# Moving group-norm sums to TensorE, a positional sum to GpSimd, and turning two matrix products around

## The chip, the cores and the metric

The kernel runs on one NeuronCore of a Trainium2 chip. Times are device microseconds of one execution. A core has five engines with a queue each: TensorE (PE in the profile, with PEld for its weight loads), VectorE (DVE), ScalarE (ACT), GpSimd (POOL) and SyncE (SP), which here issues every DMA. Each queue runs in program order, and engines wait for one another by semaphores. On-chip memory is SBUF (128 partitions) and PSUM, into which matmuls write.

## The reference, cut to what matters

The input is x, 16 images of 256 channels and 32 x 32 positions, float32. Two layers follow, each on a group-normalised input and each added to x:

```python
x = x + attention_block(_gn(x), ...)   # layer norm, 4 heads, feed-forward
x = x + mamba_block(_gn(x), ...)
```

The group norm works on the array as it is laid out in memory, with the last axis split into 16 groups of two columns: mean and variance are over all channels, all rows and the two columns of a group.

```python
g = v.reshape(B_, H_, W_, G, C_ // G)          # G = 16
m = jnp.mean(g, axis=(1, 2, 4), keepdims=True)
```

The second block adds a positional term (rel_h + rel_w), computes a gate ctx as the sigmoid of a 3-tap convolution over 256 channels, projects to u and z (512 channels each), convolves and activates u, computes delta, B and C from it, and runs a scan of 1024 steps over 512 channels with 64 states each. Then y = (ys + u * D) * silu(z), a product of y with out_proj_w gives 256 channels, and the result times ctx is taken from [position, channel] order straight into [channel, row, column] by a reshape (not by a transpose), and is added to x.

## The kernel before, in words

Channels lie on the partitions (KC = 2 blocks of 128), positions along the free axis (L = 1024, in halves of HL = 512). The scan is cut into 4096 units (256 per image): a unit is 2 channels x 64 states on 128 partitions and 1024 steps. For each unit n the main loop emits `load` (a DMA of du, broadcast, six units ahead), `inputs` (GpSimd's product with B, L956, four units ahead), pieces of `outputs` (TensorE's sums over the states, L998 and L1010, with ScalarE's copies L1004 and L1014), `scan(n)` (VectorE, L973) and `decay(n + 2)` (TensorE L965, then ScalarE's exponential L967, into a PSUM buffer of which there are two).

Everything else of the kernel is side work, woven in between the units. `prepare(b + 1)` (first norm, attention layer, scan inputs of the next image) and `gate_and_store(b - 1)` (gating, output product and store of the image before) are generators. They yield a share after every step; `rate_for` finds a rate at which the shares of one image fill its 256 units (a share below 1 isn't stretched or squeezed, and a larger one never gets below one unit). In a unit the side steps come after `scan(n)` and `decay(n + 2)`, and the last lines of the kernel fix the order of each engine's queue as it was emitted. For the first image `prepare(0)` runs before the loop, and the last `gate_and_store` runs after it. In images with both, the order of the side work is: first norm, gate_and_store, attention layer, scan inputs.

Five places matter here. `group_norm` is used twice per image, in `first_norm` and in `scan_inputs`: VectorE reduces each of the two channel blocks to 16 group sums (L274), TensorE sums these over the partitions with a constant matrix (L279), VectorE subtracts (L293), ScalarE squares (L295), the squares are summed in the same way, ScalarE turns the variance into a factor by Ln and Exp (L305, L306), and VectorE multiplies (L309). After the second norm VectorE adds the positional term (L657), and the first readers of the sum are the z products (L680). `layer_norm` (L317) already sums over channels by matmuls with a constant matrix as weights and the values as the moving operand.

`gate` computes the convolution of ctx. Its result is needed in the order of the final reshape, in which row r of the output holds four positions of 256 channels. So it takes every fourth position as the 128 columns of the weights (`xp[k][:, ds(first + t, P, 4)]`) and the 256 output channels as the moving operand, in quarters (q) of a PSUM bank, and adds the bias by a matmul of one row (L730, L736); tanh follows (L739). The output product in `gate_and_store` does the same with `us` and `wo_s` (L910), and two VectorE operations apply the gate and add x (L897, L899).

`psum` and `psum3` give PSUM banks; beside the scan there are two (`mm`) and, for `psum3`, a third (`accp`). `work` and `hwork` give SBUF tiles of 1024 and 512 columns, from 10 and 4 buffers.

## Time and profile before

| | us |
|---|---|
| median of 3 runs | 12651.92 (12599.05 to 12653.68) |
| the profiled execution | 12609.29 |
| its span, first to last instruction | 12607.5 |
| VectorE busy | 11264.3 (89%) |
| GpSimd busy | 10030.6 (80%) |
| TensorE busy, matmuls | 9517.2 (75%) |
| TensorE busy, weight loads | 5493.8 (44%) |
| ScalarE busy | 7523.0 (60%) |
| mean granted clock of TensorE | 0.799 of full |

A row of the groups reads: line, engine, operation, what it writes <- what it reads, shapes, x count | busy us, mean ns of one | idle us of the engine just before them, and what ended most of it. A row of the timeline reads: start us, duration us, engine, line, operation, x count of merged instructions, and in brackets the idle time before with its releaser. A float32 matmul has two records, so 1464 + 72 records of L730 are 768 matmuls, 48 for each of 16 images. Busy times of TensorE are modelled at their ends. A row of the waits reads: who waited <- for whom: us in total, times, the longest.

### The profile page before, as it was taken

The numbers are of one execution on the slowest core, as the hardware profiler recorded it, in microseconds if no ns is written. First come the engines' busy times: TensorE is split into PE (matmuls) and PEld (weight loads), VectorE is DVE, ScalarE is ACT, GpSimd is POOL, SyncE is SP. The second block draws the span as 40 slices with busy tenths as digits, with TensorE's granted clock in tenths as the row PEclk, the third lists the DMA queues.
The fourth block names the chain that finished last, engine by engine and source line by source line (L and its number), as shares of the span: only waits on it lengthen the run. The fifth ranks groups of instructions, "written<-read, shape, count | busy, mean of one in ns | idle before, by whom it ended". The sixth has DMA issues, their size and how long they took to land.

```text
span 12607.5 us, 421113 instructions
## 1 busy us (share of the span) xinstructions
PE 9517.2 (75%) x184752; PEld 5493.8 (44%) x184752; DVE 11264.3 (89%) x7482; ACT 7523.0 (60%) x10758; POOL 10030.6 (80%) x4201
## 2 busy tenths in 40 slices
PE   6676876868778687786878768687686877868777
PEld 2344444444444444444444444444444444444445
DVE  2799999899999899898998999999999998989998
ACT  3565655656656565565656656565565665656554
POOL 0587878878788787887878878788887878878798
PEclk7887977878878697887878878797787978878755
DMA  1566667676676766767666676766767667676676
GB/s 53 178 224 239 220 214 239 221 244 219 216 238 227 245 216 223 240 219 245 226 223 235 220 240 221 241 219 222 237 224 247 217 223 241 221 245 217 230 250 231
DMA packets 1070137, 2819.91 MB, mean 224 GB/s; under 512 B 324162, under 2 KB 402243, under 8 KB 1068292
## 3 DMA queue, kind: packets, MB, share of 16 engines
q1 hardware_dynamic: 1068292, 2792.97, 65.0%
q8 instruction: 1444, 23.66, 0.8%
q14 instruction: 401, 3.28, 0.1%
HBM read 2513.82 MB, written 261.62 MB: 220 GB/s over the span
## 4 chain that ended last, share of the span: by engine, by line
DVE 37%; PE 32%; issue 13%; ACT 8%; DMA 7%; POOL 3%; SPq 1%; DVEq 0%; POOLq 0%; ACTq 0%
DVE h L973 27%; PE yb L998 6%; PE a L965 5%; ACT a L967 4%; DMA dub<-dus 3%; PE av L531 3%; POOL dub L956 3%; PE st_ps L543 3%; DVE over L449 2%; PE z_ps L680 2%; PE s_ps L469 2%; PE g_ps L730 2%; PE yb L1010 1%; PE m_ps L910 1%; DVE u L716 1%
## 5 line engine op out<-in xcount | busy, mean ns | idle before, releaser
L956 POOL TENSOR_TENSOR dub<-dub,bt 128x1024 f32<-128x1024 f32 x4096 | 9805.4, 2420 | 2446.0 <-DMA dub<-dus 2241.7
L973 DVE TENSOR_TENSOR_SCAN h<-a,dub 128x1024 f32<-128x1024 f32 x4096 | 9176.7, 2275 | 705.4 <-ACT a L967 406.0
L967 ACT ACTIVATE a<-a,acol 128x1024 f32<-128x1024 f32 x4096 | 4464.1, 1090 | 3157.7 <-PE a L965 3092.6
L965 PE MATMUL a<-pieces,pick 48*128 48x512 bf16 x8192 | 1914.0, 458 | 2473.6 <-DVE h L973 2362.0
L998 PEld LDWEIGHTS yb<-h,cd 128*32 128x32 f32 x131072 | 2496.9, 128 | 2639.8 <-issue 1332.2
L998 PE MATMUL yb<-h,cd 128*32 128x64 f32 x131072 | 3266.9, 252 | 342.4 <-ACT y L1004 234.8
L965 PEld LDWEIGHTS <-pick 48*128 48x128 bf16 x8192 | 597.0, 95 | 2886.7 <-issue 2256.4
L1004 ACT COPY y<-yb 128x256 f32<-128x256 f32 x2048 | 763.3, 373 | 598.5 <-PE yb L998 589.1
L531 PE MATMUL av<-pt,vv 128*64 128x512 f32 x2048 | 607.7, 674 | 2.9 <-ACT sums L520 1.6
L551 ACT ACTIVATE pt<-st_ps 128x512 f32<-128x512 f32 x1024 | 552.9, 597 | 82.9 <-PE st_ps L543 82.0
L1010 PE MATMUL yb<-turn,y 128*32 128x16 f32 x32768 | 590.1, 214 | 2.3 <-issue 1.2
L543 PE MATMUL st_ps<-sp 33*128 33x512 f32 x2048 | 583.2, 646 | 2.9 <-ACT pt L551 2.9
L1010 PEld LDWEIGHTS yb<-turn,y 128*32 128x32 f32 x32768 | 571.7, 159 | 2.6 <-ACT y L1004 1.4
L730 PE MATMUL g_ps<-w,xp 128*128 128x256 f32 x1464 | 457.0, 452 | 0.1
L1014 ACT COPY yo<-yb 128x128 f32<-128x128 f32 x512 | 135.3, 264 | 519.1 <-PE yb L1010 510.9
L730 PEld LDWEIGHTS g_ps<-w,xp 128*128 128x128 f32 x1464 | 368.7, 326 | 67.7 <-issue 58.7
L469 PE MATMUL s_ps<-kd,qm 64*128 64x512 f32 x1022 | 367.5, 617 | 14.0 <-DVE kd L444 7.5
L449 DVE CUSTOM_DVE_ANT_0 over<-s_ps,over 128x512 f32<-128x512 f32 x512 | 326.8, 676 | 24.4 <-PE s_ps L469 24.4
L910 PE MATMUL m_ps<-w,xs 128*128 128x256 f32 x1024 | 321.6, 464 | 11.4 <-POOL xs L885 11.4
L716 DVE SCALAR_TENSOR_TENSOR u<-up,cwh,u 128x1024 f32<-128x1024 f32 x192 | 302.7, 1576 | 27.9 <-ACT u L708 27.7
L477 ACT ACTIVATE over<-s_ps 128x512 f32<-128x512 f32 x511 | 275.3, 595 | 32.8 <-PE s_ps L469 32.8
L910 PEld LDWEIGHTS m_ps<-w,xs 128*128 128x128 f32 x1024 | 262.9, 328 | 59.3 <-issue 26.7
(180 smaller groups left out, 7126.8 us busy)
## 6 DMA issues: line engine op xcount, KB each, us to landing
dub<-dus SPq DMA_DIRECT2D x4096, 512.0 KB
dps<-pc SPq DMA_DIRECT2D x384, 128.0 KB
pieces<-dps SPq DMA_DIRECT2D x1024, 48.0 KB
xs<-in_x_dram SPq DMA_DIRECT2D x64, 512.0 KB
xs<-kept SPq DMA_DIRECT2D x64, 512.0 KB
zs<-z SPq DMA_DIRECT2D x64, 512.0 KB
ud<-u SPq DMA_DIRECT2D x64, 512.0 KB
dus<-du SPq DMA_DIRECT2D x64, 512.0 KB
```

Of the source, the lines that this page charges most:

```text
L469: nc.tensor.matmul(s, qm[c // NJ][r, c % NJ], keys[r], start=True, stop=True)
L531: nc.tensor.matmul(av[ts(e, 2 * DH)], vv[j // (NJ // 2)][:, j % (NJ // 2), 2 * pair + e, :], pts[e], start=(j == 0), stop=(j == NJ - 1),)
L543: nc.tensor.matmul(s, ka[r, ts(j, P)], qa[r, hs(hf)], start=True, stop=True)
L730: nc.tensor.matmul(ps[:, ts(q, C)], xp[k][:, ds(first + t, P, 4)], wg_s[:, k, t, :], start=(k == 0 and t == 0), stop=False,)
L910: nc.tensor.matmul(ps[:, ts(q, C)], us[d][:, ds(first, P, 4)], wo_s[:, d, :], start=(d == 0), stop=(d == ND - 1),)
L956: nc.gpsimd.tensor_tensor(v, v, blocks[units[n][0]]["bt"], ALU.mult)
L965: nc.tensor.matmul(a[:, hs(hf)], w, pieces[r], start=True, stop=True)
L967: nc.scalar.activation(a, a, AF.Exp, scale=acol[:, at : at + 1])
L973: nc.vector.tensor_tensor_scan(now["h", e][:, i, :], decays.pop(n), loaded.pop(n), 0.0, ALU.mult, ALU.add)
L998: nc.tensor.matmul(yb[ts(g, 32), ts(s, 64)], cd[:, at // 16, ts(c, 32)], hbuf[:, :, at : at + 8], start=(c == 0), stop=(c == 1),)
L1004: nc.scalar.copy(y2[:, r], yb[:, :256])
L1010: nc.tensor.matmul(some[ts(r, 32), x], y2[:, r, x:256:8], turn[:, x], start=True, stop=True)
```

## The change

The group norm's sums are made by TensorE: a constant matrix (1 / the number of values in a group) is the weights and the values themselves move, so that a PSUM bank collects 512 column sums over all channels and both halves; one VectorE reduction over the bank then gives the 16 group values. ScalarE copies the mean back into the bank, and the constant factor moves into the matrix. The mean has a step of its own, so that the norm has ten steps in place of nine. The preload of the table set ahead of Ln is gone.

The positional sum after the second norm is issued on GpSimd.

The gate product now holds a 128 x 128 block of the gate's weights and moves 512 positions, so its result lies as [channel, position]; the bias comes in with the activation. The output product is turned around likewise, and since the result must still end in the order of the reshape, `join` multiplies projection and gate into an SBUF tile, and `turn_back` brings it to that order by matmuls with the identity, with every fourth position as weights. The eight steps of the stage alternate between projections ("p") and turns ("t").

```diff
--- before.py
+++ after.py
@@ -140,14 +140,15 @@
         assert i + n <= w
         return vec[:, o + i : o + i + n]
 
-    gate_b = const.tile([1, C], F32, name="gate_b")
-    nc.sync.dma_start(gate_b, gate_bias)
-    one_row = const.tile([1, P], F32, name="one_row")
-    nc.vector.memset(one_row, 1.0)
+    gate_b = const.tile([P, KC], F32, name="gate_b")
+    nc.sync.dma_start(gate_b, gate_bias.rearrange("o (k p) -> p (o k)", p=P))
+    nc.vector.tensor_scalar(gate_b, gate_b, 0.5, None, ALU.mult)
     ident = const.tile([P, P], F32, name="ident")
     make_identity(nc, ident)
     avg = const.tile([P, P], F32, name="avg")
     nc.vector.memset(avg, 1.0 / C)
+    share = const.tile([P, P], F32, name="share")
+    nc.vector.memset(share, 1.0 / (C * L / NG))
     eps = const.tile([P, 1], F32, name="eps")
     nc.vector.memset(eps, 1e-5)
 
@@ -269,40 +270,43 @@
 
 
     def group_norm(src, dst):
-        def sum_of(part, s, k):
-            view = part.rearrange("p (h g t) -> p g h t", g=NG, t=2)
-            nc.vector.tensor_reduce(s[:, k, :], view, AX.XY, ALU.add)
-
-        def mean_of(s, name):
-            m = psum(f"{name}_ps")[:, :NG]
-            for k in range(KC):
-                nc.tensor.matmul(m, avg, s[:, k, :], start=(k == 0), stop=(k == KC - 1))
+        def sum_of(part, sums, k):
+            for h in range(2):
+                nc.tensor.matmul(
+                    sums, share, part[:, hs(h)],
+                    start=(k == 0 and h == 0), stop=(k == KC - 1 and h == 1),
+                )
+
+        def mean_of(sums):
+            m = small.tile([P, NG], F32, name="gn_s", tag="gn_s")
+            nc.vector.tensor_reduce(
+                m, sums.rearrange("p (h g t) -> p g h t", g=NG, t=2), AX.XY, ALU.add
+            )
             return m
 
-        per = C / (C * L / NG)
-        s = small.tile([P, KC, NG], F32, name="gn_s", tag="gn_s")
+        s = psum("gn_m_ps")
         sum_of(src[0], s, 0)
         yield 1
         sum_of(src[1], s, 1)
-        m = mean_of(s, "gn_m")
-        yield 1
-        s = small.tile([P, KC, NG], F32, name="gn_q", tag="gn_s")
+        yield 1
+        m = s[:, :NG]
+        nc.scalar.copy(m, mean_of(s))
+        yield 1
         qs = []
-        nc.vector.tensor_scalar(m, m, per, None, ALU.mult)
         for k in range(KC):
             nc.vector.tensor_tensor(grouped(dst[k]), grouped(src[k]), over_group(m), ALU.subtract)
             q = work("gn_sq")
             nc.scalar.activation(q, dst[k], AF.Square)
             qs.append(q)
             yield 1
+        s = psum("gn_v_ps")
         sum_of(qs[0], s, 0)
         yield 1
         sum_of(qs[1], s, 1)
         del qs, q
-        v = mean_of(s, "gn_v")
-        yield 1
-        table("log")
-        nc.scalar.activation(v, v, AF.Ln, bias=eps, scale=per)
+        yield 1
+        v = s[:, :NG]
+        nc.scalar.activation(v, mean_of(s), AF.Ln, bias=eps)
         nc.scalar.activation(v, v, AF.Exp, scale=-0.5)
         yield 2.2
         for k in range(KC):
@@ -654,7 +658,7 @@
         )
         del xs
         for k in range(KC):
-            nc.vector.tensor_tensor(body[k], body[k], rels[k], ALU.add)
+            nc.gpsimd.tensor_tensor(body[k], body[k], rels[k], ALU.add)
             yield 0.6
         del rels
 
@@ -719,24 +723,22 @@
 
         gates = {}
 
-        def gate(o, hf, q, k):
-            if (hf, q, k) == (0, 0, 0):
+        def gate(o, hf, part):
+            if (hf, part) == (0, 0):
                 gates["g"] = work("g")
-            if (q, k) == (0, 0):
+            if part == 0:
                 gates["ps"] = psum("g_ps")
             g, ps = gates["g"], gates["ps"]
-            first = o * HL + hf * 2 + q
-            for t in range(3):
+            for at in ((0, 1), (2,), (3, 4), (5,))[part]:
+                k, t = divmod(at, 3)
                 nc.tensor.matmul(
-                    ps[:, ts(q, C)], xp[k][:, ds(first + t, P, 4)], wg_s[:, k, t, :],
-                    start=(k == 0 and t == 0), stop=False,
+                    ps, wg_s[:, k, t, ts(o, P)], xp[k][:, ds(hf * HL + t, HL)],
+                    start=(at == 0), stop=(at == 5),
                 )
-            if k < KC - 1:
-                return
-            nc.tensor.matmul(ps[:, ts(q, C)], one_row, gate_b, start=False, stop=True)
-            if q == 1:
-                table("tanh")
-                nc.scalar.activation(g[:, hs(hf)], ps, AF.Tanh, scale=0.5)
+            if part == 3:
+                nc.scalar.activation(
+                    g[:, hs(hf)], ps, AF.Tanh, scale=0.5, bias=gate_b[:, o : o + 1]
+                )
                 if hf == 1:
                     nc.sync.dma_start(gs[ts(o, P), :], g)
 
@@ -754,16 +756,16 @@
             tap(d, 2)
             table("tanh")
             nc.scalar.activation(ups[d][:, :L], us[d], AF.Tanh)
-            gate(d // 2, d % 2, 0, 0)
+            gate(d // 2, d % 2, 0)
             yield 1
-            gate(d // 2, d % 2, 0, 1)
+            gate(d // 2, d % 2, 1)
             yield 1.5
             nc.vector.scalar_tensor_tensor(us[d], ups[d][:, :L], 1.0, us[d], ALU.add, ALU.mult)
             ups[d] = None
             nc.sync.dma_start(ud[ts(d, P), :], us[d])
-            gate(d // 2, d % 2, 1, 0)
+            gate(d // 2, d % 2, 2)
             yield 1
-            gate(d // 2, d % 2, 1, 1)
+            gate(d // 2, d % 2, 3)
             yield 1.5
         gates.clear()
         del xp, body
@@ -890,35 +892,54 @@
                 yield 0.4
         if b + 2 < B:
             come += fetches(state[b + 2].setdefault("tok", []), state[b + 2]["kept"])
-        ready = []
+        turned, gated = [], {}
 
         def finish():
-            for o, hf, ps in ready:
-                nc.vector.scalar_tensor_tensor(ps, gs[o][:, hs(hf)], 1.0, ps, ALU.add, ALU.mult)
+            for o, hf, ps in turned:
                 t = xs[o][:, hs(hf)]
                 nc.vector.scalar_tensor_tensor(t, ps, 0.25, t, ALU.mult, ALU.add)
                 if hf == 1:
                     nc.sync.dma_start(out[b, ts(o, P), :], xs[o])
-            ready.clear()
-
-        for o in range(KC):
-            for hf in range(2):
-                ps = psum3("m_ps")
-                for q in range(2):
-                    first = o * HL + hf * 2 + q
-                    for d in range(ND):
-                        nc.tensor.matmul(
-                            ps[:, ts(q, C)], us[d][:, ds(first, P, 4)], wo_s[:, d, :],
-                            start=(d == 0), stop=(d == ND - 1),
-                        )
-                    if q == 1:
-                        finish()
-                    if come:
-                        come.pop(0)()
-                    yield 1.3
-                ready.append((o, hf, ps))
+            turned.clear()
+
+        def project(o, k):
+            ps = psum3("m_ps")
+            for d in range(ND):
+                nc.tensor.matmul(
+                    ps, wo_s[:, d, ts(k, P)], us[d][:, hs(o)],
+                    start=(d == 0), stop=(d == ND - 1),
+                )
+            return ps
+
+        def join(o, k, ps):
+            v = gated[o, k] = hwork("v")
+            nc.vector.scalar_tensor_tensor(v, gs[k][:, hs(o)], 1.0, ps, ALU.add, ALU.mult)
+
+        def turn_back(o, hf):
+            ps = psum3("o_t")
+            for q in range(2):
+                for k in range(KC):
+                    nc.tensor.matmul(
+                        ps[:, ds(q * C + k * P, P)], gated[o, k][:, ds(hf * 2 + q, P, 4)], ident,
+                        start=True, stop=True,
+                    )
+            turned.append((o, hf, ps))
+
+        work_on = [("p", 0, 0), ("p", 0, 1), ("p", 1, 0), ("t", 0, 0), ("p", 1, 1), ("t", 0, 1), ("t", 1, 0), ("t", 1, 1)]
+        joined = []
+        for what, o, i in work_on:
+            for j in joined:
+                join(*j)
+            joined.clear()
+            finish()
+            if what == "p":
+                joined.append((o, i, project(o, i)))
+            else:
+                turn_back(o, i)
+            if come:
+                come.pop(0)()
+            yield 1.3
         finish()
-        del ps
         yield 1
         state[b].clear()
 
```

## The prediction

> **What bounds the kernel now.** I read the page's busy shares, then the costliest groups, then groups by shape, the timeline around the changed steps, the waits, and last the busy time by stretches.
>
> ```profile
> PE 9517.2 (75%) x184752; PEld 5493.8 (44%) x184752; DVE 11264.3 (89%) x7482; ACT 7523.0 (60%) x10758; POOL 10030.6 (80%) x4201
> ...
> L973 DVE TENSOR_TENSOR_SCAN h<-a,dub 128x1024 f32<-128x1024 f32 x4096 | 9176.7, 2275 | 705.4 <-ACT a L967 406.0
> ```
>
> 4096 scans in a row are the spine: in the timeline the first begins at 426 us and the last ends at 12561 us, 2.96 us per unit, of which the scan is 2.28. Three scans back to back take 6.64 us, so a unit with nothing else costs 2.2. The rest is side work on VectorE and waiting. But VectorE is not the only chain. On TensorE's queue, unit n is: pieces of L998, then the decay L965 of unit n+2, which waits for scan n, then the side matmuls of unit n. So side matmuls delay the next decay, and with it a scan two units on. Where TensorE is at full clock the cycle outside the side matmuls is 0.84 us:
>
> ```profile
> 3588.66 0.39 PE L965 MATMUL a<-pieces,pick 48*128 48x512 bf16 x2
> ...
> 3588.97 1.95 PEld L910 LDWEIGHTS m_ps<-w,xs 128*128 128x128 f32 x8 [0.23 <-issue]
> 3588.98 2.24 PE L910 MATMUL m_ps<-w,xs 128*128 128x256 f32 x8
> ...
> 3591.74 0.39 PE L965 MATMUL a<-pieces,pick 48*128 48x512 bf16 x2
> ```
>
> From decay to decay is 3.08 us = 0.84 + 2.24. So a side step with over about 1.4 us of matmuls makes TensorE, not VectorE, set the unit. This kernel balances two engines, and the change moves work from one to the other. All sums below are per image; 15 images' side work lies in the loop.
>
> **The positional sum to GpSimd (L657).** Two steps, in one unit.
>
> ```profile
> L657 DVE TENSOR_TENSOR xp<-xp,xs x32: 1203/3224/3376, 291.3 to 11684.4; 128x1024 f32<-128x1024 f32 x32
> L611 DVE TENSOR_TENSOR xs<-xs x32: 1192/1200/2864, 269.5 to 11634.6; 128x1024 f32<-128x1024 f32 x32
> ...
> L885 POOL TENSOR_TENSOR xs<-xs x64: 2337/2344/2395, 1228.1 to 12583.8; 128x1024 f32<-128x1024 f32 x64
> ```
>
> (min/median/max ns.) L657 alone takes 1.2 us; inside the loop the median is 3.2, the same shape as L611 at 1.2. Averaged over the 15 images, the unit that holds both L657 lasts 7.46 us, against 2.49 for the mean unit without side work. Worth: 15 x 4.97 = -75 us, if GpSimd hides them. Here the Trainium skill speaks against the change: GPSIMD Engine Reference, section "Engine selection", puts an elementwise add on VectorE and calls GpSimd about 2 times slower for two inputs. The row agrees on the price (2.34 against 1.20), and by the rule alone the step loses 2 x 1.14 us an image, +34 us in all. I go by the rows: GpSimd's price is off the path, VectorE's is on it at 3.2. What is queued behind the adds on GpSimd is the products L956, 2.35 us each. In the timeline GpSimd has the product four units ahead done 3.5 us after the unit before starts, just when the second L309 ends (3.4). The two adds then end at 8.2. The first reader, L680, can start only after its decay, at about 8.3, so it waits almost nothing; the next product ends at 10.5 and its scan starts at 14. Bounds: -79 (down to 2.2 a unit) to -45 (L680 waits 2 us, and the decay behind it).
>
> **The group norms' sums.** Removed per norm: four reductions of 1.2 us, one small scaling on VectorE, and L279's four matmuls of 16 columns.
>
> ```profile
> L274 DVE TENSOR_REDUCE gn_q<-gn_sq 128x16 f32<-128x1024 f32 x64 | 76.3, 1195 | 0.0
> ...
> L317 PE MATMUL ln_m<-xs,avg 128*128 128x512 f32 x252 | 158.0, 759 | 18.1 <-DMA xs<-kept 18.1
> ```
>
> Added per norm: eight 512-column matmuls (two per step; a matmul is two records), and two reductions of 512 PSUM elements; L449, with the same operand size, takes 0.68 us; a copy of the means on ScalarE, 0.2 like L306, lies beside it. VectorE's account: 8 x 1.2 + 0.3 - 4 x 0.68 = 7.2 us an image saved, -108 us over the loop. But the nearest row for a sum step is not a reduction, it is the layer norm's mean, L317: the same constant matrix, shape and count. That, or its twin L680, looks so:
>
> ```profile
> 3237.43 4.58 DVE L657 TENSOR_TENSOR xp<-xp,xs 128x1024 f32<-128x1024 f32 x2
> ...
> 3244.81 3.74 PE L680 MATMUL z_ps<-xp,w 128*128 128x512 f32 x4
> ...
> 3249.38 1.98 PE L680 MATMUL z_ps<-xp,w 128*128 128x512 f32 x4
> ```
>
> 3.74 us first, 1.98 later. The stretches say why:
>
> ```profile
> 3206.00:3237.00 31.00, 17.91 (x412) 12.39 (x412) 30.96 (x24) 16.32 (x22) 20.47 (x9) 0.61 0.90 315
> ...
> 3244.00:3266.00 22.00, 21.73 (x298) 9.87 (x297) 19.04 (x14) 13.62 (x18) 14.23 (x7) 0.90 0.59 199
> ```
>
> (us; PE, PEld, DVE, ACT, POOL busy; granted clock; DMA share; GB/s.) The first stretch is a group norm: clock 0.61. The sums are put exactly where TensorE is slowest. The Trainium skill (TensorE: Matmul & The Clock Gate, section "Part 1") gives some 3.4 us of work before full rate and advises to neglect the ramp, under 1% of a span. Neglected, all sums cost 1.98. By the rows the first of each pair costs 3.74, four times an image: 4 x 1.76 = 7 us, as much as the whole saving. I go by the rows; by the rule the term below would be some +9 us, not +66.
>
> And the new reduction waits for the second sum, one step earlier on another queue. From scan start 0: decay ends 2.7, first sum 2.9 to 4.9 (full clock), pieces and decay, second sum 6.2 to 8.2; VectorE is through its third scan at 6.7, waits to 8.35, reduces to 9.0. Three units in 9.0; before, two units took 3.36 + 3.31 and 0.16 for the scaling = 6.83, and the one added step takes an idle unit worth 2.0 to 2.2 from elsewhere. So +0.1 at full clock, about +2 with a slow first sum. For the variance three units took 3.31 + 3.31 + 2.20 = 8.8 and will take 9.0 to 11.7. A like pair today, L631 followed by L627, confirms the wait:
>
> ```profile
> DVE xs L627 <- PE f_ps L631: 37.4, 30, 4.1
> ```
>
> 1.25 us each time. I take +2.2 us per norm, 30 norms: +66 us. Bounds: -108 (VectorE's account, all matmuls hidden) to +130 (slow clock each time). Behind the waiting reduction stand all later scans; the decays behind the sums cost what is counted. The removed table preload is no gain: an ACT_TABLE_LOAD of 1.28 us will be wanted before Ln, and perhaps one more before Exp; one at L686 may go in turn. 0 to +16, I take +5. With the longer norm, SP issues the output stage's first four loads a step earlier against the norm's end; L881 waits 147.7 us for loads in all, so this could give some back: 0, down to -15.
>
> **The gate product.** Today 48 matmuls of 256 columns and 8 of bias an image; afterwards 24 of 512. Twelve records of L730 (six take 1.78 us) plus two of L736 (0.69) become four (1.98) and two (1.1): TensorE saves 8.8 us an image. But units that hold L730 average 3.70 beside a VectorE tap and 2.24 without one: VectorE (L716, L761) sets this stage already. Worth 0; between -20 and +5.
>
> **The output product.**
>
> ```profile
> 3580.53 3.80 PE L910 MATMUL m_ps<-w,xs 128*128 128x256 f32 x8
> ```
>
> The streamed columns stay the same: 32 matmuls of 256 become 16 of 512. Today a step is bound by its weight loads (8 x 0.244 = 1.95 from the row above), so eight steps take 8 x 2.24 = 17.9 us and 1.5 for a slow start. A projection step afterwards streams 8 records of 0.43 (L680's 1.98 = 4 x 0.43 + 0.27): 3.7 us. A turning step still loads 128 columns at stride 4 eight times: 2.24. 4 x 3.7 + 4 x 2.24 = 23.8: **+5.9 us an image on TensorE**, in a stage where TensorE already sets the units (ten units from the first L910 take 32.4 us, VectorE's own part is 10 x 2.2 + 4 x 1.37 = 27.5). VectorE's count stays eight operations of 0.68. But each join now waits for a projection issued only a step before: 0.6 + 3.7 us after the decay, against a scan of 2.28. Followed through as above, the stage takes about 39.5 us: +7. Fourteen images: +98; the last two, one spread thin and one after the last scan: +12. Sum +110, bounds +40 (idle units absorb it) to +140.
>
> **Sum.** -75 + 66 + 5 + 0 + 110 = +106 us. The profiled execution took 12609.3 us (span 12607.5, some 2 us around it), inside the runs' 12599 to 12654; I carry the difference to the median: 12651.9 + 106 = 12758, told as **12755 us**.
>
> **Rivals.** (1) Even: idle units between steps absorb half of TensorE's excess, sums +15, output +55, L657 -75: 12647. For it speaks that decays run two units ahead; against it, that the 15 steps in question follow one another almost without gaps. (2) Faster: VectorE, busy 89%, is the bound and its account holds: -75 - 108 + 40: 12509. It needs sums hidden wholly; the point is 1.4 us of side matmuls per unit, and a sum has 1.98 at best. (3) Much slower: TensorE is slow in all sum pairs and in the first projections, and L680 waits for GpSimd: -45 + 130 + 16 + 140: 12893.
>
> **How the numbers follow.** Likeliest (TensorE sets the new steps) 0.58, own range 12690 to 12850; even 0.22; faster 0.12; much slower 0.08. About 0.5% is what can be told from no change: 12589 and 12715. Below: the faster case, 0.12. Between: the even case and 0.06 of the likeliest's low end, 0.28. Above: 0.60. The range leaves out the faster case and the worst: 12600 to 12860.
>
> **What would show it.** Right: no VectorE add at the old L657 and its unit near 2.5 us; the sum matmuls at 3 to 3.7 us first, 2 later; VectorE's busy time down by some 180 us while its idle time before the new reduction and the join grows to over 200; the stage of outputs at 39 us. Wrong: reductions that find their sums ready, joins without waiting, or L680 waiting for GpSimd for microseconds.

## The result and the profile after

The changed kernel takes 12578.6 us (median of 10 runs, 12556.9 to 12604.9), the kernel before 12621.7 in the same comparison (10 runs, 12568.2 to 12654.4). The ratio is 0.9968 with a 95% interval of 0.9949 to 0.9987: some 40 us less, where 12755, about 106 us more, was forecast. The forecast stood on 12651.9, a median of three, so 30 us of the distance to 12755 lie in its base. The profiled execution took 12592.9, its span 12590.8.

From the page of the changed kernel, the busy shares and two groups (busy us, mean ns | idle before, releaser):

```profile
PE 9574.8 (76%) x183984; PEld 5140.4 (41%) x183984; DVE 11064.3 (88%) x7355; ACT 7506.0 (60%) x10792; POOL 10050.9 (80%) x4233
...
L994 DVE TENSOR_TENSOR_SCAN h<-a,dub 128x1024 f32<-128x1024 f32 x4096 | 9166.7, 2273 | 596.0 <-ACT a L988 314.3
...
L661 POOL TENSOR_TENSOR xp<-xp,xs 128x1024 f32<-128x1024 f32 x32 | 75.1, 2349 | 254.1 <-DVE xp L313 246.5
```

VectorE lost 200 us of busy time and the span lost 17. The waits of VectorE in the changed kernel show where much of it turned into waiting (us, times, longest):

```profile
DVE v L916 <- PE m_ps L908: 139.7, 58, 5.2
...
DVE gn_s L282 <- PE gn_v_ps L275: 97.2, 31, 5.4
DVE gn_s L282 <- PE gn_m_ps L275: 93.7, 33, 6.5
```

These 331 us are the waits that the prediction named: the join for its projection, the new reduction for its sum. The timeline of the changed kernel shows one of each, first the mean of a first norm, then the start of an output stage (start us, duration, engine, line, bracket: idle time and releaser):

```profile
2698.33 6.08 PE L275 MATMUL gn_m_ps<-xs,share 128*128 128x512 f32 x8
...
2704.45 0.69 DVE L282 TENSOR_REDUCE gn_s<-gn_m_ps 128x16 f32<-128x512 f32 x1 [4.40 <-PE gn_m_ps L275]
```

```profile
2766.02 6.37 PE L908 MATMUL m_ps<-xs,w 128*128 128x512 f32 x8
...
2772.42 0.69 DVE L916 SCALAR_TENSOR_TENSOR v<-xs,m_ps 128x512 f32<-128x512 f32 x1 [4.82 <-PE m_ps L908]
...
2777.76 3.70 PE L908 MATMUL m_ps<-xs,w 128*128 128x512 f32 x8
...
2781.50 0.69 DVE L916 SCALAR_TENSOR_TENSOR v<-xs,m_ps 128x512 f32<-128x512 f32 x1 [1.65 <-PE m_ps L908]
...
2782.30 2.13 PE L922 MATMUL o_t<-ident,v 128*128 128x128 f32 x8
```

A later projection has 3.70 us and a turn 2.13, as forecast (3.7 and 2.24). In the first norm both mean sums run in one go, eight records in 6.08 us, and the reduction stands 4.40 us. In a second norm they are quick:

```profile
3165.89 1.98 PE L275 MATMUL gn_m_ps<-xs,share 128*128 128x512 f32 x4
...
3168.71 1.98 PE L275 MATMUL gn_m_ps<-xs,share 128*128 128x512 f32 x4
...
3170.73 0.69 DVE L282 TENSOR_REDUCE gn_s<-gn_m_ps 128x16 f32<-128x512 f32 x1 [0.80 <-PE gn_m_ps L275]
```

The stretches show the clock in which each ran (the third number from the right):

```profile
2698.30:2704.40 6.10, 6.10 (x14) 2.44 (x16) 1.75 (x1) 1.09 (x1) 6.10 (x3) 0.60 1.01 329
2766.00:2772.40 6.40, 6.40 (x15) 2.52 (x17) 1.60 (x1) 1.09 (x1) 6.40 (x3) 0.58 1.02 365
3158.00:3165.00 7.00, 5.28 (x164) 3.28 (x153) 7.00 (x7) 2.82 (x4) 5.58 (x3) 1.00 0.68 208
3165.80:3170.70 4.90, 4.90 (x48) 2.02 (x50) 4.13 (x2) 2.45 (x3) 1.72 (x1) 1.00 1.01 370
```

The first norm's mean sums and the first projection had 0.60 and 0.58 of the full clock. The second norm's had all of it, as had the stretch just ahead of them, in which the feed-forward product ends.

So what was expected to get slower did. Something else got faster. To find it I cut each image at the scan during which a stage's first instruction starts, and took the mean over images 1 to 14 (us per image; worked out of the scans' starts in the timelines; the single parts are experiments told of below):

| stage | before | after | add alone | gate alone | outputs alone | norms alone | empty step |
|---|---|---|---|---|---|---|---|
| first norm | 34.3 | 42.2 | 34.3 | 34.3 | 34.3 | 42.0 | 37.6 |
| gating | 31.6 | 29.1 | 31.8 | 31.6 | 31.6 | 29.3 | 30.3 |
| outputs | 32.4 | 37.9 | 32.3 | 32.3 | 36.8 | 32.1 | 32.0 |
| layer norm, q, k, maxima | 148.7 | 149.1 | 149.5 | 149.2 | 148.6 | 150.7 | 149.6 |
| softmax | 157.7 | 153.0 | 159.5 | 157.8 | 159.0 | 153.6 | 152.9 |
| output projection, feed-forward | 57.8 | 59.0 | 58.5 | 58.2 | 57.8 | 57.9 | 57.4 |
| second norm with the add | 40.7 | 34.9 | 35.5 | 40.7 | 40.5 | 35.2 | 35.2 |
| z | 24.7 | 23.6 | 25.4 | 24.9 | 25.0 | 25.7 | 25.8 |
| taps and gate | 92.5 | 92.9 | 94.6 | 90.1 | 90.7 | 90.4 | 92.0 |
| scan inputs | 148.4 | 147.0 | 148.5 | 147.2 | 148.4 | 147.7 | 148.1 |
| image | 768.9 | 768.7 | 769.9 | 766.3 | 772.7 | 764.7 | 761.0 |

First norm and outputs cost 13.4 us more, the second norm gives 5.8 back, as steps foresaw. But the softmax, which no edit touches, gives 4.7, and it does so only in the columns in which each norm has one step more. About half of that is a matter of counting: there the softmax begins at unit 81 of the image in place of 80, and ends at 141 as before, so it holds one idle unit of 2.2 us less, the one that the prediction let the step take. The rest is time: units 81 to 135, into which no less work falls, take 2.3 us less in the changed kernel (two profiles of the kernel before differ by 1.0 there). Over the 14 images these cancel almost to nothing (-0.2 each). The span's 17 us lie outside: the first scan starts 12 us earlier, image 0 takes 15.5 less, image 15 and the tail 14 more. A second profile of the program before also has its first scan 14 us earlier, so the 12 need not come from the edit. By the stages, gain and loss cancel but for little.

### The profile page after: what moved, and what is told of

It is laid out like the page before. It is cut to its first block, busy times and chain, and to the rows that moved or that the text cites. A ratio compares the mean times of both kernels' runs of the same rounds, so it can differ in the third digit from the quotient of the medians.

```text
span 12590.8 us, 419601 instructions
## 1 busy us (share of the span) xinstructions
PE 9574.8 (76%) x183984; PEld 5140.4 (41%) x183984; DVE 11064.3 (88%) x7355; ACT 7506.0 (60%) x10792; POOL 10050.9 (80%) x4233
## 4 chain that ended last, share of the span: by engine, by line
DVE 37%; PE 31%; issue 13%; ACT 8%; DMA 7%; POOL 3%; SPq 1%; DVEq 0%; POOLq 0%; ACTq 0%
DVE h L994 28%; PE a L986 5%; PE yb L1019 5%; ACT a L988 4%; DMA dub<-dus 3%; POOL dub L977 3%; PE av L535 2%; DVE over L453 2%; PE st_ps L547 2%; PE m_ps L908 2%; PE z_ps L684 2%; PE s_ps L473 2%; DMA xs<-ud 2%; DVE u L720 1%; PE gn_v_ps L275 1%
## 5 line engine op out<-in xcount | busy, mean ns | idle before, releaser
L986 PE MATMUL a<-pieces,pick 48*128 48x512 bf16 x8192 | 1875.8, 448 | 2444.5 <-DVE h L994 2333.4
L1019 PEld LDWEIGHTS yb<-h,cd 128*32 128x32 f32 x131072 | 2433.3, 126 | 2822.9 <-issue 1601.6
L1019 PE MATMUL yb<-h,cd 128*32 128x64 f32 x131072 | 3189.4, 248 | 341.0 <-ACT y L1025 203.3
L734 PE MATMUL g_ps<-xp,w 128*128 128x512 f32 x732 | 406.9, 668 | 0.0
L473 PE MATMUL s_ps<-kd,qm 64*128 64x512 f32 x1022 | 340.6, 612 | 21.2 <-DVE kd L448 14.6
L453 DVE CUSTOM_DVE_ANT_0 over<-s_ps,over 128x512 f32<-128x512 f32 x512 | 325.9, 671 | 24.7 <-PE s_ps L473 24.4
L908 PE MATMUL m_ps<-xs,w 128*128 128x512 f32 x504 | 279.2, 704 | 10.2 <-POOL xs L887 9.4
L706 PE MATMUL u_ps<-xp,w 128*128 128x512 f32 x512 | 280.0, 674 | 1.5 <-ACT u L712 1.4
L661 POOL TENSOR_TENSOR xp<-xp,xs 128x1024 f32<-128x1024 f32 x32 | 75.1, 2349 | 254.1 <-DVE xp L313 246.5
```

What stands on the lines that cost most here:

```text
L453: nc.vector.tensor_tensor_reduce(r, s, r, 1.0, -3.0e38, ALU.add, ALU.max, mx[:, at : at + 1])
L473: nc.tensor.matmul(s, qm[c // NJ][r, c % NJ], keys[r], start=True, stop=True)
L986: nc.tensor.matmul(a[:, hs(hf)], w, pieces[r], start=True, stop=True)
L1019: nc.tensor.matmul(yb[ts(g, 32), ts(s, 64)], cd[:, at // 16, ts(c, 32)], hbuf[:, :, at : at + 8], start=(c == 0), stop=(c == 1),)
```

## Experiments

**The parts alone.** Theory A was that the terms of the forecast are right one by one but GpSimd gives part back; the rivals, that one part is mis-sized, or that the edits help each other.

The add:

```diff
-            nc.vector.tensor_tensor(body[k], body[k], rels[k], ALU.add)
+            nc.gpsimd.tensor_tensor(body[k], body[k], rels[k], ALU.add)
```

> The kernel before with one part of the change: the positional sum after the second norm on GpSimd, all else as before. Theory (VectorE's 3.2 us additions leave the path and GpSimd's wait is small): -75 us, bounds -79 to -45, ratio 0.994. Rival (the z products wait for GpSimd and hand the delay to the decays): 0 to -20 us. Rival (the gain is larger because later stages profit): beyond -90 us.

Measured 0.9991 (0.9981 to 1.0000), 11 us less. The stage of the norm and the add falls by 5.3 us per image, more than the 4.97 of the forecast. But the timeline of this kernel shows what stands behind the two adds on GpSimd:

```profile
3203.07 4.65 POOL L657 TENSOR_TENSOR xp<-xp,xs 128x1024 f32<-128x1024 f32 x2
...
3207.66 18.58 POOL L956 TENSOR_TENSOR dub<-dub,bt 128x1024 f32<-128x1024 f32 x8
```

Eight products without a gap, 2.32 us each: GpSimd catches up during the z stage. In all 14 images it has done so 10 to 16 us before the first tap, so the late products themselves never meet the taps. Yet there VectorE's operations with two SBUF inputs take longer: L716 1668 ns on average in place of 1576, L761 1868 in place of 1732. Taps, z and softmax give back 4.6 us per image. The same place with the add left out on every engine tells whether this is the cause:

```diff
-            nc.vector.tensor_tensor(body[k], body[k], rels[k], ALU.add)
```

> The kernel before with the positional sum left out on every engine (the second block then works without it; the loads of the term stay). Theory A (the 5.3 us per image that GpSimd's additions saved in their own unit are given back because GpSimd falls 4.7 us behind with its products): without the additions nothing falls behind, -60 to -80 us. Theory B (whatever shortens that unit is given back, since what VectorE loses is its operations with two SBUF inputs waiting for GpSimd's product in flight, and those of the next stages then meet it instead): -25 to 0 us, and the taps' stage longer by 1 to 2 us per image.

Measured 0.9943 (0.9930 to 0.9957), 71 us less; the taps take 91.8, L716 1564 ns and L761 1670. So VectorE's release is worth what the forecast said, 71 for 75, and having the adds on GpSimd takes 60 of it back (some 20 either way). Longer runs of L716 and L761 are 33 of the 60. How adds that were caught up with before still change when the taps meet products was not isolated.

The gate, the output stage and the norms (with their tenth step), each with the changed lines of the diff alone:

> The kernel before with the gate product alone turned around (weights held, bias in the activation), and the output stage left as before, so the gate is applied in the wrong order of positions; its instructions are the same in number and shape. Theory of the prediction (VectorE sets the gate's units): 0, between -20 and +5 us. Rival (TensorE's lag behind the gate reaches the steps after it, whose stage is 2.7 us shorter per image in the changed kernel, and the stretch ahead of the loop is bound by TensorE): -35 to -60 us.

Measured 0.9954 (0.9937 to 0.9971), 58 us less.

> The kernel before with the output stage alone turned around (projections, joins, turns); the gate is made as before, so it is joined in the wrong order of positions. Theory (TensorE has 5.9 us more to do per image and the joins wait): +110 us by the prediction, +85 to +100 us by the stage as it is in the changed kernel (5.5 us for each of 14 images, about 10 us at the end). Rival (the stage is hidden by idle units): under +40 us.

Measured 1.0040 (1.0026 to 1.0053), 50 us more, the output stage +4.4 per image.

> The kernel before with the group norms' sums alone on TensorE. Theory of the prediction (waits for the second sum, one step more per norm): +66 us. Rival (the step more takes an idle unit out of stages that TensorE sets, where it is worth 2.4 us or more, and the earlier loads of the output stage give back 2.5 us per image): -30 to +10 us. Rival (VectorE's account): -100 us.

Measured 0.9960 (0.9947 to 0.9974), 50 us less. The first norm takes 7.7 us longer per image; what pays for it lies elsewhere: the softmax at 153.6, the second norm with its add at 35.2, the taps at 90.4. The four parts alone come to -69 us, the whole change to -40.

How far do the stages of one program repeat?

> The kernel before, unchanged, for a second profile: how far stages and VectorE's operations with two SBUF inputs differ between two executions of one program. If the gains and losses of the stage with the taps in the single-part kernels (92.5 us per image before, 90.1 to 94.6 there) are chance from execution to execution, this one will lie anywhere in 90 to 95 us too; if they come from the programs, it will lie within 1 us of 92.5, and the softmax stage (157.7) within 1 us as well.

12615.0 us, with the stages within 0.6 us of the first profile's (softmax 158.1 for 157.7). The softmax's -4.7 is no chance.

**The empty step.** The norms alone hold two edits, the sums and one step more. So the kernel before got the step alone, twice per image, without any work in it:

```diff
         m = mean_of(s, "gn_m")
         yield 1
+        yield 1
```

> The kernel before with one empty step more in each group norm, behind the mean, as the changed kernel has it there, and nothing else. Theory of the prediction (a step taken from elsewhere is worth just the idle unit that it adds): 0 us within 15. Rival (the step takes a unit out of the softmax and its followers that costs more than the 2.2 us it adds, and the output stage's loads go out a step sooner): -35 to -60 us, with the softmax stage near 153 us and the gating stage near 29.

Measured 0.9901 (0.9887 to 0.9914): 125 us less, 12487. A step that does nothing is worth more than all the edits, and this kernel beats both. Against it the sums proper cost 0.9960 - 0.9901, or 74 us (some 24 either way), near the forecast's +66. The other parts were put on it, and the whole change was run without it, both mean sums in one step:

> The kernel before with the empty step in each norm and the positional sum on GpSimd. With the empty step alone the additions on VectorE have fallen from 2.6 to 1.6 us each, so there is less to win. Theory (GpSimd's backlog costs about 60 us wherever it falls): -125 - 35 + 60, so -90 to -110 us. Rival (the two add up as measured alone): -136 us, and up to -160.

0.9935 (0.9909 to 0.9961), so the add on GpSimd costs 43 us here, where the step has spread the adds already (some 37 either way; by the profiles 2.4 us per image).

> The kernel before with the empty step in each norm and the gate product turned around, the output stage as before (so the gate is applied in the wrong order of positions). Theory (the 58 us that the gate product won alone is TensorE's lag that it takes off the stages behind the gate): -165 to -190 us. Rival (a good part of it was VectorE's taps meeting GpSimd's products less often, which depends on where steps fall): -115 to -150 us.

0.9871 (0.9843 to 0.9899), 162 us less; 37 of the gate's 58 stay (some 39 either way, which settles neither theory; by the profiles 2.0 us per image).

```diff
         sum_of(src[0], s, 0)
-        yield 1
         sum_of(src[1], s, 1)
```

> The changed kernel with nine steps in a norm, as before the change: both sums of the mean are issued in one step. Theory (the added step's shift of all later steps is what the prediction left out; without it the forecast of +106 us over the kernel before holds): +60 to +110 us over the kernel before. Rival (the step matters little in the whole, where the other parts have moved things anyway): -50 to +10 us.

1.0077 (1.0051 to 1.0103), 97 us more, the softmax back at 159.3. So without the step more, the change costs about the +106 of the forecast. But the terms do not add up to it: add, gate and outputs alone come to -19 us (-11 - 58 + 50), which leaves 116 for the norms in nine steps, and these were not run by themselves. More steps are not better:

```diff
         sum_of(src[1], s, 1)
         yield 1
+        yield 1
...
         del qs, q
         yield 1
+        yield 1
```

> The group norms' sums alone on TensorE, with one more empty step between the second sum and the reduction that reads it, both for mean and variance. Theory (VectorE's waits of 93 and 96 us for the second sum are lost time, and steps are cheap): the waits go to under 30 us and the time falls by 60 to 120 us more than with the sums alone, to -110 to -170 us. Rival (TensorE's lag behind the sums delays the decays anyway, so the wait only moves to the scans): -30 to -70 us, as with the sums alone.

1.0096 (1.0080 to 1.0111), 121 us more: a clear miss. The waits for the sums did fall, from 189 us to 52, and the time rose all the same. I had taken the waits for the loss and a step as their cure.

**What is it about the step?** An added step does three things: it gives the norm room, it moves every later stage by a unit against the groups of eight units in which `outputs` works, and it raises the pace of all longer shares. The pace alone:

```diff
-            rate, due = rate_for(total, UNITS - AHEAD - 3), 0.0
+            rate, due = rate_for(total, UNITS - AHEAD - 5), 0.0
```

> The kernel before with two units taken from the room that the side work of an image is spread over, in place of two empty steps: all steps above one unit are squeezed as by the added step, but the norms and the loads of the output stage stay where they were. Theory (it is the new spacing of the later steps that wins): -70 to -130 us, with the softmax stage near 153 us. Rival (it is the step's own place and the earlier loads): -20 to +20 us.

1.0025 (1.0007 to 1.0043). Not the pace alone: the softmax stays at 158.6, and the taps take 95.4. Then the step in one norm only, in both at the old pace, and one step outside the norms, ahead of the output product:

> The kernel before with the empty step after the mean in the first norm alone; nothing computed is changed. Place (the stages from the output product to the softmax come one unit later against the groups of eight units): most of the gain of both steps, since these stages are moved here as there, -80 to -130 us. Rate (each added step raises the pace of the side work by half as much): about half, -60 us. Room (a norm gains by a free unit between its mean and its subtraction): about half, -60 us, and the first norm alone no longer than one idle unit more (37 us).

> The kernel before with the empty step in the second norm alone; nothing computed is changed. Place: the stages ahead of the second norm stand where they stood, the softmax stays at 157 to 159 us per image, and little is gained, -50 to +30 us. Rate: half, -60 us. Room: half, -60 us, with the second norm at 35 to 36 us in place of 40.8.

```diff
-            rate, due = rate_for(total, UNITS - AHEAD - 3), 0.0
+            rate, due = rate_for(total, UNITS - AHEAD - 1), 0.0
```

> The kernel before with the empty step in both norms, and two units more of room in the rate, so that the pace of the long steps stays nearly that of the kernel before; nothing computed is changed. Place: -60 to -160 us, with the softmax at 151 to 154 us per image. Room: -100 to -130 us. Rate: nothing is left, -20 to +20 us.

```diff
             come += fetches(state[b + 2].setdefault("tok", []), state[b + 2]["kept"])
+        yield 1
         ready = []
```

> The kernel before with one empty step per image just ahead of the output product, and none in the norms; nothing computed is changed. Place: the output product and what follows it come one unit later, the softmax takes 151 to 154 us per image, -70 to -160 us. Rate: half, -60 us. Room: no gain, 0 to +30 us.

Measured 1.0023 (1.0012 to 1.0034), 1.0019 (1.0007 to 1.0030), 1.0010 (0.9994 to 1.0026) and 1.0037 (1.0022 to 1.0052). Not one of these gains, so none of the three theories holds by itself. The gain lies in how step, place and pace come out together, and the traces show a good part of how. After the softmax the sums go to memory and back, a reciprocal is taken on VectorE, and its result goes the same way. The kernel before, image 3 (SPq: a transfer being issued):

```profile
3132.26 0.55 SPq L568 DMA_DIRECT2D few<-den  x1
...
3135.91 0.33 DVE L575 RECIPROCAL few<-few 128x32 f32<-128x32 f32 x1
3136.62 0.55 SPq L577 DMA_DIRECT2D den<-few  x1
...
3145.49 0.96 DVE L587 TENSOR_TENSOR ao<-ao,sums 128x512 f32<-128x512 f32 x1 [0.57 <-DMA sums<-den]
```

The kernel with the step in the first norm alone, image 3:

```profile
3120.76 0.55 SPq L570 DMA_DIRECT2D few<-den  x1
...
3124.78 0.35 DVE L577 RECIPROCAL few<-few 128x32 f32<-128x32 f32 x1 [2.48 <-DMA few<-den]
...
3130.25 1.04 SPq L582 DMA_DIRECT2D sums<-den  x2
...
3137.01 2.19 DVE L589 TENSOR_TENSOR ao<-ao,sums 128x512 f32<-128x512 f32 x1 [3.19 <-DMA sums<-den]
```

There VectorE stands twice for a transfer. The unit with the reciprocal lasts 5.5 us on average and the one with the first product 7.8, against 3.1 and 4.5 before (scan start to scan start). The steps there have shares of 0.5, and a share below 1 isn't stretched: whether three such steps fill one unit or two depends on the fraction at which the count of shares arrives. I walked the shares of each kernel: from the load to the reciprocal there are three units in the kernel before and with the empty step in both norms, two with the step in the first norm, in the second, or ahead of the output product. In the miss with more steps there are two as well, and the units last 5.4 and 7.4. With both at the old pace the reciprocal has three, and only the product's unit is long, 7.4. There the transfer of the result comes one unit later and falls behind the two stores (ys<-yo) that `outputs` issues once in eight units:

```profile
3097.03 0.35 DVE L577 RECIPROCAL few<-few 128x32 f32<-128x32 f32 x1
3097.59 1.21 SPq L1023 DMA_DIRECT2D ys<-yo  x2
3098.85 0.58 SPq L579 DMA_DIRECT2D den<-few  x1
...
3110.59 0.85 DVE L589 TENSOR_TENSOR ao<-ao,sums 128x512 f32<-128x512 f32 x1 [4.52 <-DMA sums<-den]
```

From the end of the reciprocal to that issue 1.4 us pass on average, in the kernel before 0.1.

The fraction decides over the add's two steps of 0.6 too. In the kernel before both fall into one unit (the prediction shows them, 4.58 us together); with the empty step in both norms:

```profile
3164.73 1.61 DVE L658 TENSOR_TENSOR xp<-xp,xs 128x1024 f32<-128x1024 f32 x1
...
3166.26 2.28 DVE L974 TENSOR_TENSOR_SCAN h<-a,dub 128x1024 f32<-128x1024 f32 x1
...
3168.47 1.19 DVE L658 TENSOR_TENSOR xp<-xp,xs 128x1024 f32<-128x1024 f32 x1
```

One in each; the two units take 7.5 us, where before the full unit and its successor took 9.6. With the norms' part alone they take 6.8.

A stage's time hides this where the stage gains or loses a unit. So here is the change against the kernel before by fixed unit numbers (us per image, mean over images 1 to 14; the softmax's transfers and products lie in 136 to 149, the second norm, the add and z in 162 to 179):

| units | 0 to 80 | 81 to 135 | 136 to 149 | 150 to 161 | 162 to 179 | 180 to 255 | image |
|---|---|---|---|---|---|---|---|
| kernel before | 249.2 | 139.3 | 40.3 | 40.4 | 58.8 | 241.0 | 768.9 |
| its second profile | +0.4 | +1.0 | 0.0 | 0.0 | -0.1 | +0.1 | +1.3 |
| changed kernel | +9.2 | -2.3 | 0.0 | -2.8 | -3.3 | -1.1 | -0.2 |
| step in both norms | +0.4 | -2.8 | +0.3 | -0.6 | -4.5 | -0.9 | -7.9 |
| in the first alone | +0.9 | -2.3 | +5.8 | -1.3 | +1.0 | -1.0 | +3.1 |
| in the second alone | +0.2 | -3.0 | +7.4 | -0.4 | 0.0 | -0.7 | +3.4 |
| in both, old pace | +0.1 | -0.3 | +3.1 | -0.5 | +0.4 | -0.7 | +2.0 |
| ahead of the output product | +1.2 | -1.4 | +6.3 | -1.3 | +1.1 | -1.7 | +4.2 |
| pace alone | +0.1 | +3.3 | +2.0 | +0.9 | -3.6 | +0.9 | +3.6 |

Up to unit 80 the empty step costs next to nothing. The four kernels whose step gained nothing lose it in 136 to 149, by the waits shown; these outweigh what they gain in 81 to 135. The last row is a warning: by the walk the pace alone also leaves three units to the reciprocal and parts the adds, and yet it lost. From the output projection on its stages begin one to three units earlier, so its columns hold in part other work; but the two fractions are not all.

Two runs test this reading (the first expectation counts only the units in between, and so says two where I say three). One changes nothing but the fraction, by half a unit of room; the other takes the step ahead of the output product, which lost, and only sets the fraction right:

```diff
-            rate, due = rate_for(total, UNITS - AHEAD - 3), 0.0
+            rate, due = rate_for(total, UNITS - AHEAD - 3.5), 0.0
```

> The kernel before with half a unit less room in the rate, 1.1690 in place of 1.1645, and no step more; nothing computed is changed. Worked out from the shares: every stage begins at the unit where it began, give or take one, the softmax at unit 80, two units lie between the load of the sums of the softmax and their reciprocal as before, but the two steps of the positional sum fall into two units and no longer into one. Fractions (short steps that share a unit or do not): the two adds take 3.8 us a unit in place of 7.5 for both in one, so -2.4 us per image, -35 us (-20 to -60). Steps in the norms, or the place of the softmax, as the only cause: 0 (-15 to +15).

```diff
             come += fetches(state[b + 2].setdefault("tok", []), state[b + 2]["kept"])
+        yield 1
         ready = []
...
-            rate, due = rate_for(total, UNITS - AHEAD - 3), 0.0
+            rate, due = rate_for(total, UNITS - AHEAD - 3.8), 0.0
```

> The kernel before with one empty step per image ahead of the output product, as in the run before that had it, and a rate of about 1.181 in place of 1.1736; no step more in a norm; nothing computed is changed. Worked out from the shares: the output product at unit 18 and the softmax at 81 as there, but three units between the load of the softmax's sums and their reciprocal in place of two, and the two adds in two units. Fractions together with place: the units of the reciprocal and of the first product with it fall from 5.4 and 7.8 us to about 3.2 and 4.2, -5.8 us per image, the adds give -2.4 to -3.5 more, so from +41 us to about -80 to -100 against the kernel before. Room inside the norms as the cause of the gain: no gain, 0 to +50.

Measured 0.9973 (0.9963 to 0.9983), 34 us less for 35, and 0.9957 (0.9940 to 0.9973), 54 us less. The second moved from +47 to -54 by its pace alone. The reciprocal and product of that kernel:

```profile
3085.34 0.33 DVE L575 RECIPROCAL few<-few 128x32 f32<-128x32 f32 x1
...
3090.00 1.71 SPq L580 DMA_DIRECT2D sums<-den  x4
...
3094.44 1.39 DVE L587 TENSOR_TENSOR ao<-ao,sums 128x512 f32<-128x512 f32 x1
```

No wait in either; their units last 3.3 and 3.9 us, as expected. Three things came out otherwise. The two units of the adds take 8.8 us in both kernels, not 7.6, so in the first of them this explains 0.8 of some 2.3 us per image, and the match of 34 with 35 is partly luck. The second reached -54, not -80 to -100: units 180 to 208, the taps and the gate, take 95.7 us there, for 91.9 with the same step at the old pace. L716 and L761 take 1597 and 1989 ns on average there, for 1447 and 1568; that they fall otherwise between GpSimd's products is the likely reason, not a shown one. And neither reaches the empty step's -125.

What is shown: fractions of a unit move this kernel by 30 to 100 us, in good part through named waits. The place counts too: in units 81 to 99 the ten kernels here whose softmax begins at unit 81 take 0.3 to 1.8 us less per image than the kernel before, and all that begin at 80, its second profile among them, 0.1 to 1.1 more. What stays open: why that is so, and what lengthens the taps. Unit 95 lasts over 4 us in 8 of 14 images before, in 12 of 14 in the second profile, and in none with the empty step in both norms; the link to the groups of eight is argued from this, and was not isolated.

## Why the prediction was wrong, by its own steps

- **"The one added step takes an idle unit worth 2.0 to 2.2 from elsewhere": the price was right, what comes behind was left out, and that decided.** Up to unit 80 the empty step costs 0.4 us per image, as the prediction had it. But it put the effect on all later stages at nothing, without a reason. The empty step takes 2.8 us per image off units 81 to 135 and 4.5 off the second norm, the add and z, and is worth -125 us in all (0.9901). I costed a step by the time of a unit and never asked where all later steps would land. Walking the shares by hand, which needs no more than the yields and the rate, shows that the adds part into two units. It would not have shown the gain in 81 to 135.
- **The norms' sums, +66 (-108 to +130): right.** +74 against the kernel with the empty step. The split was not as told: the first norm costs 4.6 us against the empty step's (42.2 for 37.6), nearly all of the 74 over 15 images, the second 0.6 less than with the step and the add on GpSimd (34.9 for 35.5). Two steps start in the first unit of an image, so both mean sums of the first norm run there together, at 0.60 of the clock; the second norm's have the full clock, 1.98 us each in 13 of 14 images, where the prediction had the first of every pair slow. The variance's sums took 3.75 and 2.02 us in the second norm, as said. The Trainium skill puts the ramp at under 1% of a typical span (TensorE: Matmul & The Clock Gate, "Part 1"). With the ramp neglected the prediction made this term +9; 74 were measured, so the rows were the better guide.
- **The add, -75: the mechanism right, the cover wrong.** VectorE's release is worth 71 with the add left out, 11 with it on GpSimd. The forecast followed the products only to the first scan behind the adds, found it in time, and stopped. GpSimd, with products of 2.35 us in units of 2.2 to 3, was late for eight of them, and z, the taps and the next softmax got longer; by which path, stays open. The Trainium skill's rule that I set aside (GPSIMD Engine Reference, "Engine selection": an elementwise add on VectorE) would have made it +34, and came out nearer: -11 alone, +43 on top of the empty step. Its factor of two, 2.35 for 1.20 us, is not where the 60 us went.
- **The gate, 0 (-20 to +5): wrong in size,** -58 alone. I reasoned that VectorE sets this stage, so that TensorE's 8.8 us lie beside (9.4 by the rows that the prediction names; TensorE's busy time fell by 7.5 per image). VectorE's own part is not fixed: with the new gate L716 takes 1395 ns on average for 1576, and the stage fell by 2.4 us per image. That the taps meet fewer products because TensorE's queue is shorter there is argued, and was not isolated.
- **The outputs, +110 (+40 to +140): right in kind, too large.** The stage took 37.9 us for the 39.5 forecast, and +50 alone. Steps of 3.7 and 2.13 us were as worked out; what took up the rest was not isolated. The last two images cost 14 us more, for the 12 said.
- **Table loads, +5, and loads a step earlier, 0: small, as said.** 83 loads of tables for 81, but two of 1.28 us now stand in each second norm ahead of the factor; the wait for loads in the gating fell from 147.7 to 105.4 us.

Against the parts alone, the add came out 64 us worse than its term, the gate 58 and the outputs 60 better, and the norms with their step 116 better (-50 for +66). The last is the largest. That the form with nine steps lies so near the forecast (+97 for +106) is in part luck. Of the rivals, "even" came nearest as a change (-5 us, measured -40), but not for its reason: the 331 us of waits show that idle units did not absorb TensorE's excess; what changed behind the added step paid for it.

## What to carry to other kernels

Where side work is woven into a loop at a computed pace, an edit that adds or removes a step moves all steps behind it: walk the shares of both versions and compare which short steps share a unit and which stand between a transfer's issue and its reader, ahead of any sum over durations. To judge such an edit, give the old kernel the step without the work; only the difference to that belongs to the work. Moving work to an engine in the shadow of another is not free just because its queue catches up in time: here it had caught up 10 us before the stage that got longer. Leave the work out on every engine; the difference to that is what its new place costs.

## What the runs showed of the hardware

A VectorE operation with two SBUF inputs waits for a GpSimd product in flight. Of the 30 adds L657 in the loop of the kernel before, 29 begin while a product runs and end 1.08 us after that product's end. An add took 1.20 us at the least, 3.38 at the most, and 1.61 on average where the pace spreads it. The Trainium skill (SBUF — State Buffer, "SBUF: two separate sides") says that the two engines share a pair of ports as an exclusive lock held for a whole instruction; this fits, 3.38 - 1.20 being nearly a product's 2.35. What I had not expected is how far this may go: the mean of the 192 taps moved between 1355 and 1668 ns from kernel to kernel with their code unchanged, 60 us of VectorE's time. That this too comes from where they fall between products is argued.

The pace of TensorE's sums followed the clock that it was granted: in one second norm the four records of the first variance sum took 3.76 us at 0.52 of full, those of the next 1.98 us at 1.00.

The round trip of the softmax's sums through memory is hidden or not by one unit: the unit with the reciprocal takes 5.1 to 5.5 us where two units lie between the load and its use, and 2.9 to 3.5 where there are three.
